# Two transformer layers on one core: which units of the second attention are projected early, in what order the units run, and how the reciprocals of the softmax sums are spread

## The chip, the core and the metric

The kernel runs on one core of one Trainium2 chip. The metric is the device time of one launch in microseconds (us). A core has a matrix engine (PE, with its weight loads shown as PEld), a vector engine (DVE), a scalar engine (ACT), GpSimd (POOL), and SyncE (SP), which here only issues transfers. Each engine runs its instructions in its own order, and they wait for each other by semaphores. Transfers between HBM and the core's memory are issued by SP, ACT or POOL and carried by 16 DMA engines.

## The reference

Everything is fp32. `x` has 8 sequences of 100 tokens with 512 features (800 tokens), the context `ctx` 8 sequences of 722 rows. The two layers, cut to what matters:

```python
# layer 0: attention, 16 heads of 32, causal; keys and values from ctx[:, :100]
y  = softmax(mask(q k^T / sqrt(32))) v ;  x = y @ o_w + o_b (+ the residual)
# FFN 0: layer norm, router over 8 experts, the two best per token
x  = x + sum_of_two( w_e * (gelu(xn W1_e + b1_e) W2_e + b2_e) )
# layer 1: attention, 16 heads of 64; mem = ctx @ Wm serves as keys AND as values
xn = layernorm(x);  q = xn @ Wq;  k, v = split(xn @ Wkv)
k  = concat(k, heads(ctx @ Wm));  v = concat(v, heads(ctx @ Wm))
x  = softmax(q k^T / 8) v @ Wo + bo (+ the residual)
# FFN 1: router over 8 experts, two best, silu(gate) * up, down; then a layer norm
```

In layer 1 each query of 100 sees 100 own keys and 722 projected ones, 822 in all. The product `ctx @ Wm` does not depend on x: it can be computed at any time.

## The kernel before

**Stages.** The 800 tokens lie in 7 tiles of 128 rows. Attention 0 (L445 to 594) runs 32 units (4 groups of four heads times 8 sequences) with keys and scores one unit ahead (`weighed0`, L493; `turned0`, L514; `attended0`, L522), then the output product L585, the residual, the layer norm factors and the router's logits tile by tile. `places` (L218) works out where each token's row goes among the experts' rows, `owners` (L285) reads the experts' order into registers of SP, `by_order` (L291) sorts the biases by that order on DVE (L295, L300). `send` (L303) scatters 14 half tiles of rows from POOL to the HBM table `sent`. FFN0 (`work_off`, L365) fetches the rows of each expert (`xg`, L329), transposes them (L151), multiplies (L656, L341) and writes to the HBM table `answers`; `fetch` (L315, L317) brings each token's two rows back.

**Projections.** A unit of attention 1 is a sequence b and a pair of heads ic (64 units). Its projected memories are mT (128 features by 722), made by `context_columns` (L406: 8 products in two halves of 361, 16 records in the trace at L411, then two ACT copies L415), and mv, the same transposed back by `context_rows` (L417, L423). For the units in EARLY (L32), five each of b = 0 and 1, this is done ahead by `project_early` (L435): those of b = 0 after the routing of FFN0, while the tokens are sent, those of b = 1 after FFN0, while the answers are fetched. The results go to HBM (`kept_keys`, `kept_values`) on ACT's queue. Wm and the context for b = 0 are loaded by SP after routing into tiles of attention 0 that are done with (L609, L611), those for b = 1 by POOL at FFN0's start (`fetch_context`, L637).

**Attention 1** begins with the layer norm and the transposes of its 7 tiles (a loop after the fetch loop), then the queries (L400) and per half the keys (L807). The units then run in order of b and ic, one unit ahead in the scores:

- `keys` (L723) computes mT or, for a kept unit, reads it from HBM by SP; next to a kept unit the first half of the following late one is computed with it;
- `turned` (L766) transposes the probabilities of the unit before, and a POOL copy L782 spreads its reciprocals over 128 columns (`wide`);
- `values` (L734) computes or reads mv;
- `weighed` (L742) makes the scores (L752), the maxima on DVE (L756), exponentials with their sums on ACT (L758), and the reciprocals of the sums (L763);
- `attended` (L785) finishes the unit before: PE transposes `wide` (L788) so that the reciprocals lie along the columns, the 14 pairs of products with mv and v follow (L794), ACT copies the reciprocals out of PSUM (`over`, L796), and DVE multiplies by them (L797).

**What sets the order.** The weights come through a ring of eight 1 MB buffers (class `Weights`, L44): `load(n)` issues on SP the next pieces of a fixed list, in the order of the list, and each waits for its buffer. With `behind`, a one-element POOL copy ties a load to another tile. Within each engine a scheduler arranges instructions by their dependences and its own priorities; buffers go round in pools (the number `bufs` each), and a new tile waits for the readers of the old one in its place.

Of the kernel before, what the change touches and what calls it, by code (L numbers as in the profile page):

```python
# [8 lines left out]
F32 = mybir.dt.float32  # L9
# [4 lines left out]
P = 128  # L14
# [17 lines left out]
EARLY = ((0, 1, 3, 5, 7), (0, 1, 3, 5, 7))  # L32
KEPT = {(b, ic): (b * len(EARLY[0]) + k) for b in range(len(EARLY)) for k, ic in enumerate(EARLY[b])}

# [9 lines left out]
class Weights:  # L44


    def __init__(self, nc, pool, pieces):
        self.nc, self.pool, self.pieces, self.tiles = nc, pool, pieces, []

    def load(self, n, behind=None):  # L50

        while len(self.tiles) < min(n, len(self.pieces)):
            t = self.pool.tile([P, 4, 512], F32, tag="w", name=f"w{len(self.tiles)}")
            piece = self.pieces[len(self.tiles)]
            if behind is not None:
                self.nc.gpsimd.tensor_copy(t[:1, 0, :1], behind[:1, 0, :1])
            self.nc.sync.dma_start(out=t, in_=piece() if callable(piece) else piece)
            self.tiles.append(t)
# [7 lines left out]
def two_layers(ctx: ExitStack, tc: tile.TileContext, a: dict, out: bass.AP):  # L66
# [8 lines left out]

    pieces = [a[n] for n in ("k_w", "q_w", "v_w", "o_w")]
    W_L0F = len(pieces)
# [8 lines left out]
    pieces += [a["Wq"][g] for g in range(2)] + [a["Wkv"][g] for g in range(4)]  # L86
    pieces += [a["Wm"][g] for g in range(2)] + [a["Wo"][g] for g in range(2)]
# [127 lines left out]
    kept_keys = dram.tile([len(KEPT), P, S], F32, name="kept_keys")  # L215
    kept_values = dram.tile([len(KEPT), P, NSC, P], F32, name="kept_values")
# [74 lines left out]
    def by_order(hot, src, n, pool, name):  # L291

        shape = [P, NE, n, NE]
        wide = pool.tile(shape, F32, tag=f"o_{name}", name=f"o_{name}")
        nc.vector.tensor_tensor(  # L295
# [69 lines left out]
    def work_off(jobs, arrive, hidden, product, send_back, first=None, midway=None):  # L365
# [3 lines left out]
        if first is not None:  # L369
            weights.load(first + 8, raw)  # L370
# [35 lines left out]
    def context_columns(mT, ic, cb, w_m, psum, tag, halves=(0, 1)):  # L406

        for h in halves:
            pm = psum.tile([P, 512], F32, tag=tag, name="ps_m")
            for dc in range(DC):  # L410
                nc.tensor.matmul(  # L411
                    pm[:, : S // 2], w_m[ic // 4][:, dc, (ic % 4) * P : (ic % 4 + 1) * P],
                    cb[:, dc, h * (S // 2) : (h + 1) * (S // 2)], start=dc == 0, stop=dc == DC - 1,
# [21 lines left out]
    def project_early(b, cb, w_m, tiles, psum, tags):  # L435
        for ic in EARLY[b]:
            mT, mv = tiles()
            context_columns(mT, ic, cb, w_m, psum, tags[0])
            nc.scalar.dma_start(out=kept_keys[KEPT[b, ic]], in_=mT)
            context_rows(mv, mT, psum, tags[1], nc.scalar.copy)  # L440
            moved(nc.scalar.dma_start, mv, kept_values[KEPT[b, ic]], True)
# [4 lines left out]
    with tc.tile_pool(name="a0", bufs=1) as ap, tc.tile_pool(name="a0w", bufs=3) as aw, tc.tile_pool(  # L446
# [19 lines left out]
        for t in (sent, answers):  # L466
            for r0, r1 in ((0, sum(CAPS)), (sum(CAPS), ROWS)):
                flat = t[r0:r1].rearrange("r d -> (r d)").rearrange("(p f) -> p f", p=P)
                n = (r1 - r0) * D // P
                for k in range(0, n, 1024):  # L470
                    if t is sent or r0:
                        nc.sync.dma_start(out=flat[:, k : min(n, k + 1024)], in_=nil[:, : min(1024, n - k)])

        xT = ap.tile([P, DC, NT], F32, tag="xT", name="xT0")
# [69 lines left out]
        prs, prTs = {}, {}  # L544
        for n in range(len(units) + 2):
            if n < len(units):
# [25 lines left out]
        xT = ap.tile([P, DC, NT], F32, tag="xT", name="xTf0")  # L572
# [31 lines left out]
        weights.load(W_L0F + 2)  # L604
        send(xl, where, "f0")
        w_m = []
        for g, tag in enumerate(("cT", "kT")):
            w_m.append(ap.tile([P, 4, 512], F32, tag=tag, name=f"wm0{g}"))
            nc.sync.dma_start(out=w_m[g], in_=a["Wm"][g])  # L609
        cb = ap.tile([P, DC, S], F32, tag="v", name="cb0")  # L610
        nc.sync.dma_start(out=cb, in_=a["ctxT"][:, 0, :].rearrange("(c p) s -> p c s", p=P))  # L611
        project_early(
            0, cb, w_m, lambda: (
                ap.tile([P, S], F32, tag="nil", name="mT0", bufs=2), aw.tile([P, NSC, P], F32, tag="xn", name="mv0")
            ), ps, ("tp", "av"),
        )
        b1s = by_order(hot, b1.rearrange("p e f -> p f e"), F0 // P, fp, "b1")
        b2s = by_order(hot, b2T, DC, fp, "b2")
# [386 lines left out]
```

## Time and profile before

| | |
|---|---|
| median of 3 runs (lowest, highest) | 1885.26 us (1885.07, 1887.0) |
| the profiled execution | 1887.75 us |
| its span in the trace | 1886.0 us |
| mean granted clock of PE | 0.952 |
| PE busy, matmuls of it at L411 | 1744.2 us, 277.6 us (864 records) |
| DVE, ACT, POOL busy | 576.5, 468.3, 161.7 us |
| moved by DMA | 225.15 MB, 119 GB/s over the span |

The stages by their place in the span (us): head 0 to 41, attention 0 to 158, its output and logits to 203, routing and early projections to 238, wait for FFN0's rows to 255, FFN0 to 639, fetching back with early projections to 680, layer norm to 698, queries and keys to about 780, units of attention 1 to about 1480, FFN1 to 1822, output.

How to read the lines: L12 is line 12 of the kernel. A line of a timeline gives the start, the length of a run of alike instructions, engine, line, operation, result and operands, shape, count, and in brackets how long the engine had been idle and what released it. Matmuls are pipelined, so a run's own length overlaps the next; the distance of two starts is what a slot costs. A row of stages gives busy time and count by engine, the granted clock (1.00 is full), the share of DMA time and GB/s.

### The profile page before, as it was taken

The page shows a single profiled execution, that of the slowest core. Times are in us where ns is not written, and L with a number is a line of the kernel's source. Part 1 is how long each engine was busy: PE and PEld are TensorE (multiplying, and loading weights), DVE is VectorE, ACT ScalarE, POOL GpSimd, SP SyncE. Part 2 cuts the span into 40 slices and gives each one's busy share as a digit, 9 for nine tenths or more (in the row PEclk, how much of TensorE's full clock was granted, in tenths as well). Part 3 has the DMA queues.
Part 4 walks back from the last instruction along what each step waited for, and adds up shares of the span by engine and source line. Part 5 has one row for each costly group of instructions (what it writes and reads, how often), then busy time and mean ns, then how long its engine had stood idle before and what let it go on. Part 6 is the DMA issues. An engine that isn't in the chain of part 4 may idle for free. (4 is left out here: it accounts for less than half of the span.)

```text
span 1886.0 us, 26129 instructions
## 1 busy us (share of the span) xinstructions
PE 1744.2 (92%) x10442; PEld 1318.2 (70%) x10442; DVE 576.5 (31%) x1379; ACT 468.3 (25%) x1389; POOL 161.7 (9%) x281
## 2 busy tenths in 40 slices
PE   5999969999999879999999999999999939999990
PEld 2455559999999745666666666666666428999990
DVE  4465300101111140355444234444443321111115
ACT  2374311111111141343333323333332010010110
POOL 4010110000000130000000000000000140000003
PEclk9997879999999979999999999999999859999995
DMA  9701284464556552032000000000000056555523
GB/s 368 313 24 55 108 317 164 177 248 174 201 205 231 196 176 79 24 95 72 1 32 1 32 1 32 1 33 1 1 1 1 12 199 224 183 181 203 206 89 113
DMA packets 51883, 225.15 MB, mean 119 GB/s; under 512 B 8336, under 2 KB 10008, under 8 KB 35104
## 3 DMA queue, kind: packets, MB, share of 16 engines
q1 hardware_dynamic: 32440, 169.51, 24.8%
q0 software_dynamic: 10064, 32.15, 4.8%
q10 hardware_dynamic: 9240, 21.65, 3.2%
q8 instruction: 86, 1.41, 0.3%
q14 instruction: 53, 0.43, 0.1%
HBM read 176.76 MB, written 46.53 MB: 118 GB/s over the span
## 5 line engine op out<-in xcount | busy, mean ns | idle before, releaser
L341 PE MATMUL ps_y<-h,w 128*128 128x256 f32 (+7 forms) x1536 | 280.5, 344 | 0.0
L411 PE MATMUL ps_m<-cb,w 128*128 128x361 f32 x864 | 277.6, 472 | 0.0
L341 PEld LDWEIGHTS ps_y<-h,w 128*128 128x128 f32 x1536 | 268.6, 190 | 7.9
L411 PEld LDWEIGHTS ps_m<-cb,w 128*128 128x128 f32 x864 | 158.9, 189 | 95.4 <-issue 3.6
L656 PE MATMUL ps_h<-xgT,w 128*128 128x256 f32 (+7 forms) x1024 | 189.9, 347 | 0.0
L656 PEld LDWEIGHTS ps_h<-xgT,w 128*128 128x128 f32 x1024 | 181.0, 192 | 6.0
L758 ACT ACTIVATE pr<-ps_sc,m 100x822 f32<-100x822 f32 x128 | 120.0, 943 | 192.6 <-DVE m L756 192.6
L774 DVE COPY prT<-ps_ptA 128x500 f32<-128x500 f32 x128 | 82.2, 678 | 197.1 <-PE ps_ptA L773 197.1
L756 DVE TENSOR_REDUCE m<-ps_sc 100x1 f32<-100x822 f32 x128 | 123.8, 1009 | 47.2 <-PE ps_sc L752 47.2
L660 ACT ACTIVATE h<-ps_h,s_b 128x256 f32<-128x256 f32 (+7 forms) x128 | 56.2, 439 | 315.6 <-PE ps_h L656 315.6
L415 ACT COPY mT<-ps_m 128x361 f32<-128x361 f32 x128 | 59.0, 462 | 252.1 <-PE ps_m L411 224.3
L400 PE MATMUL ps_col<-xT,w 128*128 128x400 f32 x320 | 115.3, 519 | 0.0
L884 PE MATMUL ps_g<-xgT,w 128*128 128x256 f32 (+7 forms) x512 | 104.6, 348 | 0.0
L884 PE MATMUL ps_u<-xgT,w 128*128 128x256 f32 (+7 forms) x512 | 103.1, 344 | 0.0
L400 PEld LDWEIGHTS ps_col<-xT,w 128*128 128x128 f32 x320 | 61.9, 197 | 46.2 <-issue 4.6
L884 PEld LDWEIGHTS ps_g<-xgT,w 128*128 128x128 f32 x512 | 91.4, 192 | 3.0
L884 PEld LDWEIGHTS ps_u<-xgT,w 128*128 128x128 f32 x512 | 91.1, 191 | 2.8
L752 PE MATMUL ps_sc<-mT,qT 64*100 64x311 f32 (+1 forms) x512 | 91.9, 466 | 0.0
L889 ACT ACTIVATE sg<-ps_g 128x256 f32<-128x256 f32 (+7 forms) x64 | 22.3, 349 | 239.3 <-PE ps_g L884 239.3
L782 POOL COPY wide<-sums 100x128 f32<-100x128 f32 x64 | 18.8, 294 | 728.1 <-DVE sums L763 728.1
L890 DVE TENSOR_TENSOR h<-ps_u,sg 128x256 f32<-128x256 f32 (+7 forms) x64 | 24.4, 381 | 184.2 <-PE ps_u L884 152.9
L794 PE MATMUL ps_av<-prT,mv 128*64 128x100 f32 (+1 forms) x1536 | 80.6, 253 | 0.0
(240 smaller groups left out, 1964.0 us busy)
## 6 DMA issues: line engine op xcount, KB each, us to landing
w<-in_W SPq DMA_DIRECT2D x64, 1024.0 KB
w<-in_w_gate SPq DMA_DIRECT2D x16, 1024.0 KB
w<-in_w_up SPq DMA_DIRECT2D x16, 1024.0 KB
w<-in_w_down SPq DMA_DIRECT2D x16, 1024.0 KB
sent<-nil SPq DMA_DIRECT2D x25, 512.0 KB
cb<-in_ctxT ACTq DMA_DIRECT2D x8, 1444.0 KB
answers<-nil SPq DMA_DIRECT2D x19, 512.0 KB
xg<-sent POOLq DMA_DIRECT2D x18, 256.0 KB, 4.8
```

The lines of the kernel that those rows point to most:

```text
L341: nc.tensor.matmul(py[:, k, :n], ws[f // 4][:, f % 4, dc * P : (dc + 1) * P], h[:, f, :n], start=f == 0, stop=f == nf - 1,)
L400: nc.tensor.matmul(ps[:, :HALF], w[c // 4][:, dc, (c % 4) * P : (c % 4 + 1) * P], xT[:, dc, cols], start=dc == 0, stop=dc == DC - 1,)
L411: nc.tensor.matmul(pm[:, : S // 2], w_m[ic // 4][:, dc, (ic % 4) * P : (ic % 4 + 1) * P], cb[:, dc, h * (S // 2) : (h + 1) * (S // 2)], st ...
L415: nc.scalar.copy(mT[:, h * (S // 2) : (h + 1) * (S // 2)], pm[:, : S // 2])
L656: nc.tensor.matmul(ph[:, :n], w[:, dc, j * P : (j + 1) * P], xg[:, dc, :n], start=dc == 0, stop=dc == DC - 1,)
L660: nc.scalar.activation(h[:, f, :n], ph[:, :n], AF.Gelu, bias=b1s[:, e, f : f + 1])
L752: nc.tensor.matmul(sc[:, bank, c0:c1], qT[r, ic, q0 : q0 + T], keys_, start=True, stop=True)
L756: nc.vector.tensor_reduce(m, sc[:, :, :NKH], AX.XY, ALU.max, negate=True)
L758: nc.scalar.activation(pr.rearrange("p (a n) -> p a n", a=2), sc[:, :, :NKH], AF.Exp, bias=m, accum_out=sums[:, j : j + 1],)
L774: nc.vector.tensor_copy(prT[:, : NSC - 1, :], pt)
L794: nc.tensor.matmul(po[r, 0, :], vj, prT[j][:w, c, :], start=c == 0, stop=c == NSC)
L884: nc.tensor.matmul(p_[:, :n], w_[:, dc, j * P : (j + 1) * P], xg[:, dc, :n], start=dc == 0, stop=dc == DC - 1,)
```

## The change

1. EARLY has 14 units, all 8 of b = 0 and 6 of b = 1, so 50 units are projected in attention 1 where 54 were.
2. `project_early` becomes a generator of three steps per unit (two halves of mT, then mv with the stores). Ten steps of b = 0 are taken in the last ten turns of attention 0's loop, the other 14 after routing. Its stores go to SP's queue. Its inputs are four pieces of the weight ring, loaded at the start.
3. For b = 1, Wm comes from the ring too (order now Wq, Wm, Wkv, Wo); a limit keeps the ring from loading Wkv until the last answers have been fetched. POOL fetches the context in two halves.
4. The layer norm and transposes of attention 1 stand in the loop that fetches FFN0's answers, and the transposed x has a pool of its own.
5. `by_order` is tied behind the places of the second choice by a POOL copy.
6. The reciprocals go through HBM: SP writes the 100 by 2 sums to `shares`, the two heads apart, and reads each back spread over 64 partitions (`over`). The POOL copy, the PE transpose and the ACT copy go.
7. Kept mT and mv are read by POOL's queue.
8. The units run as b = 0 and 2 in turn, then 1 and 3 in turn, then b = 4 to 7; `batch` remembers its context tile, keys and values by b and loads no context for b = 0.

```diff
@@ -29,8 +29,8 @@
...
-EARLY = ((0, 1, 3, 5, 7), (0, 1, 3, 5, 7))
-KEPT = {(b, ic): (b * len(EARLY[0]) + k) for b in range(len(EARLY)) for k, ic in enumerate(EARLY[b])}
+EARLY = ((0, 1, 2, 3, 4, 5, 6, 7), (0, 1, 3, 5, 6, 7))
+KEPT = {u: k for k, u in enumerate((b, ic) for b in range(len(EARLY)) for ic in EARLY[b])}
...
     pieces = [a[n] for n in ("k_w", "q_w", "v_w", "o_w")]
+    W_EARLY = len(pieces)
+    pieces += [a["Wm"][g] for g in range(2)] + [context(0, h) for h in range(2)]
...
-    pieces += [a["Wq"][g] for g in range(2)] + [a["Wkv"][g] for g in range(4)]
-    pieces += [a["Wm"][g] for g in range(2)] + [a["Wo"][g] for g in range(2)]
+    pieces += [a[n][g] for n in ("Wq", "Wm") for g in range(2)]
+    pieces += [a["Wkv"][g] for g in range(4)] + [a["Wo"][g] for g in range(2)]
...
+    shares = dram.tile([B * IC, 2, T], F32, name="shares")
...
-    def by_order(hot, src, n, pool, name):
+    def by_order(hot, src, n, pool, name, behind):
 
         shape = [P, NE, n, NE]
         wide = pool.tile(shape, F32, tag=f"o_{name}", name=f"o_{name}")
+        nc.gpsimd.tensor_copy(wide[:1, 0, 0, :1], behind[:1, :1])
...
-    def project_early(b, cb, w_m, tiles, psum, tags):
+    def project_early(b, cb, w_m, tiles, psum, tags, dma):
+
         for ic in EARLY[b]:
             mT, mv = tiles()
-            context_columns(mT, ic, cb, w_m, psum, tags[0])
-            nc.scalar.dma_start(out=kept_keys[KEPT[b, ic]], in_=mT)
+            for h in range(2):
+                context_columns(mT, ic, cb, w_m, psum, tags[0], (h,))
+                yield
+            dma(out=kept_keys[KEPT[b, ic]], in_=mT)
             context_rows(mv, mT, psum, tags[1], nc.scalar.copy)
-            moved(nc.scalar.dma_start, mv, kept_values[KEPT[b, ic]], True)
+            moved(dma, mv, kept_values[KEPT[b, ic]], True)
+            yield
...
+        weights.load(W_L0F)
...
+        steps = project_early(
+            0, weights.tiles[W_EARLY + 2 : W_L0F], weights.tiles[W_EARLY : W_EARLY + 2], lambda: (
+                ap.tile([P, S], F32, tag="nil", name="mT0", bufs=2), aw.tile([P, NSC, P], F32, tag="xn", name="mv0")
+            ), ps, ("tp", "av"), nc.sync.dma_start,
+        )
         for n in range(len(units) + 2):
+            if n >= len(units) - B:
+                next(steps)
...
         weights.load(W_L0F + 2)
+        for _ in steps:
+            pass
+        b1s = by_order(hot, b1.rearrange("p e f -> p f e"), F0 // P, fp, "b1", where[1])
+        b2s = by_order(hot, b2T, DC, fp, "b2", where[1])
         send(xl, where, "f0")
-        w_m = []
-        for g, tag in enumerate(("cT", "kT")):
-            w_m.append(ap.tile([P, 4, 512], F32, tag=tag, name=f"wm0{g}"))
-            nc.sync.dma_start(out=w_m[g], in_=a["Wm"][g])
-        cb = ap.tile([P, DC, S], F32, tag="v", name="cb0")
-        nc.sync.dma_start(out=cb, in_=a["ctxT"][:, 0, :].rearrange("(c p) s -> p c s", p=P))
-        project_early(
-            0, cb, w_m, lambda: (
-                ap.tile([P, S], F32, tag="nil", name="mT0", bufs=2), aw.tile([P, NSC, P], F32, tag="xn", name="mv0")
-            ), ps, ("tp", "av"),
-        )
-        b1s = by_order(hot, b1.rearrange("p e f -> p f e"), F0 // P, fp, "b1")
-        b2s = by_order(hot, b2T, DC, fp, "b2")
...
-        cb = fp.tile([P, DC, S], F32, tag="xl", name="cb1")
+        cb = fp.tile([P, 2, DC, S // 2], F32, tag="xl", name="cb1")
...
-            for t, src in (
-                (w_m[0], a["Wm"][0]), (w_m[1], a["Wm"][1]),
-                (cb, a["ctxT"][:, 1, :].rearrange("(c p) s -> p c s", p=P)),
-            ):
-                nc.gpsimd.tensor_copy(t[:1, 0, :1], behind[:1, 0, :1])
-                nc.gpsimd.dma_start(out=t, in_=src)
+            for h in range(2):
+                nc.gpsimd.tensor_copy(cb[:1, h, 0, :1], behind[:1, 0, :1])
+                nc.gpsimd.dma_start(out=cb[:, h], in_=context(1, h))
...
+        weights.limit = W_L1A + 4
...
+        bo = fw.tile([P, D], F32, name="bo", bufs=1)
+        nc.scalar.dma_start(out=bo, in_=a["bo"][0].partition_broadcast(P))
+        for _ in project_early(
+            1, [cb[:, h] for h in range(2)], [weights.get(W_L1A + 2 + g, 0) for g in range(2)], lambda: (
                 fw.tile([P, S], F32, tag="xgT", name="mT1"), fw.tile([P, NSC, P], F32, tag="xg", name="mv1")
-            ), ps, ("m", "tp"),
-        )
+            ), ps, ("m", "tp"), nc.scalar.dma_start,
+        ):
+            pass
+        xT1 = columns_tile("xT1")
...
                 nc.vector.scalar_tensor_tensor(
                     x[:w, i, :], y[:w], m[:w, i : i + 1], x[:w, i, :], ALU.mult, ALU.add
                 )
+            xn = fw.tile([P, D], F32, tag="y", name="xn1")
+            scaled(xn, x[:, i, :], *factors(moments(x[:, i, :], "a1"), "b", twice=True))
+            to_columns(xT1, xn, i * P, rows[i], ps, gamma1, beta1)
+            nc.gpsimd.tensor_tensor(x[:, i, :], x[:, i, :], bo, ALU.add)
+        weights.limit = len(pieces)
+        weights.load(W_L1A + 8, y[:1, :1])
...
-        weights.load(W_L1A + 8)
-        xT = ap.tile([P, DC, NT], F32, name="xT1")
-        with tc.tile_pool(name="a1l", bufs=2) as lp:
-            bo = lp.tile([P, D], F32, name="bo", bufs=1)
-            nc.scalar.dma_start(out=bo, in_=a["bo"][0].partition_broadcast(P))
-            for i in range(NTILE):
-                xn = lp.tile([P, D], F32, tag="xn", name="xn1")
-                scaled(xn, x[:, i, :], *factors(moments(x[:, i, :], "a1"), "b", twice=True))
-                to_columns(xT, xn, i * P, rows[i], ps, gamma1, beta1)
-                nc.gpsimd.tensor_tensor(x[:, i, :], x[:, i, :], bo, ALU.add)
-
+        xT = xT1
...
             if (b, ic) in KEPT:
-                nc.sync.dma_start(out=mT, in_=kept_keys[KEPT[b, ic]])
+                nc.gpsimd.dma_start(out=mT, in_=kept_keys[KEPT[b, ic]])
...
             if (b, ic) in KEPT:
-                moved(nc.sync.dma_start, mv, kept_values[KEPT[b, ic]], False)
+                moved(nc.gpsimd.dma_start, mv, kept_values[KEPT[b, ic]], False)
...
             nc.vector.reciprocal(sums, sums)
-            return prs, sums
-
-        def turned(prs, sums):
+            share, over = shares[b * IC + ic], small.tile([P, T], F32, tag="over", name="over1")
+            nc.sync.dma_start(out=share.rearrange("j t -> t j"), in_=sums)
+            for r, j in zip(rows_, range(2)):
+                nc.sync.dma_start(out=over[r], in_=share[j].partition_broadcast(H1))
+            return prs, over
+
+        def turned(prs, over):
...
-            wide = small.tile([T, 2, H1], F32, tag="wide", name="wide1")
-            nc.gpsimd.tensor_copy(wide, sums.unsqueeze(2).to_broadcast([T, 2, H1]))
-            return out, wide
-
-        def attended(b, ic, v, mv, prT, wide):
-
-            po = ps.tile([P, 2, T], F32, tag="tp", name="ps_av1")
-            nc.tensor.transpose(po[:, 1, :], wide.rearrange("t j d -> t (j d)"), ident[:T, :T])
+            return out, over
+
+        def attended(b, ic, v, mv, prT, over):
+
+            po = ps.tile([P, T], F32, tag="tp", name="ps_av1")
             for c in range(NSC + 1):
                 w = min(P, S - c * P) if c < NSC else T
                 for j in range(2):
                     r = slice(j * H1, (j + 1) * H1)
                     vj = mv[:w, c, r] if c < NSC else v[:, ic * P + j * H1 : ic * P + (j + 1) * H1]
-                    nc.tensor.matmul(po[r, 0, :], vj, prT[j][:w, c, :], start=c == 0, stop=c == NSC)
-            over = small.tile([P, T], F32, tag="over", name="over1")
-            nc.scalar.copy(over, po[:, 1, :])
-            nc.vector.tensor_tensor(qT[:, ic, b * T : (b + 1) * T], po[:, 0, :], over, ALU.mult)
-
...
+                    nc.tensor.matmul(po[r, :], vj, prT[j][:w, c, :], start=c == 0, stop=c == NSC)
+            nc.vector.tensor_tensor(qT[:, ic, b * T : (b + 1) * T], po, over, ALU.mult)
...
+        shared = {}
...
+            if b in shared:
+                return shared[b]
+            cb = None
+            if any((b, ic) not in KEPT for ic in range(IC)):
+                cb = aw.tile([P, 2, DC, S // 2], F32, tag="cb", name="cb")
+                for h in range(2):
+                    nc.scalar.dma_start(out=cb[:, h], in_=context(b, h))
+                cb = [cb[:, h] for h in range(2)]
...
                 nc.vector.tensor_copy(v[:, g * 512 : (g + 1) * 512], pv)
-            return cb, kT, v
-
-        before = kT = None
-        for n in range(B * IC):
-            b, ic = divmod(n, IC)
-            if ic == 0:
-                cb, kT, v = batch(b, kT)
+            shared[b] = cb, shared["kT", half], v
+            return shared[b]
+
+
+        units = [(b + 2 * k, ic) for b in range(2) for ic in range(IC) for k in range(2)]
+        units += [(b, ic) for b in range(4, B) for ic in range(IC)]
+        before = None
+        for n, (b, ic) in enumerate(units):
+            cb, kT, v = batch(b)
             mT = keys(b, ic, cb)
-            if (b, ic) in KEPT and ic + 1 < IC and (b, ic + 1) not in KEPT:
-                keys(b, ic + 1, cb, whole=False)
+            if (b, ic) in KEPT and n + 1 < len(units) and units[n + 1] not in KEPT:
+                b_, ic_ = units[n + 1]
+                keys(b_, ic_, batch(b_)[0], whole=False)
```

## The prediction

> **What bounds the kernel now.** First the page's busy shares, then the span cut into its stages, last the timelines of the stages that the change touches. In the first line PE is busy 92% of the span; no other engine passes 31%. In the stages (columns: length, busy time of PE, its weight loads, DVE, ACT, POOL, granted clock, DMA share, GB/s) the work that sets the time shows where PE fills the whole stretch: attention 1 does (895 to 1425). Not filled: 238 to 255, where PE waits 17 us for FFN0's first rows, and 673 to 710, the way from FFN0 to attention 1.
>
> ```profile
> PE 1744.2 (92%) x10442; PEld 1318.2 (70%) x10442; DVE 576.5 (31%) x1379; ACT 468.3 (25%) x1389; POOL 161.7 (9%) x281
> ```
>
> ```profile
> 203.00:238.00 35.00, 34.15 (x128) 21.18 (x128) 11.90 (x58) 10.86 (x26) 10.52 (x11) 0.87 0.47 171
> 238.00:255.00 17.00, 2.64 (x12) 2.27 (x12) 2.12 (x7) 2.20 (x4) 6.83 (x16) 0.55 0.76 281
> ...
> 673.00:710.00 37.00, 24.95 (x82) 15.40 (x82) 12.01 (x30) 15.66 (x45) 8.93 (x8) 0.72 0.44 155
> ...
> 895.00:1425.00 530.00, 530.00 (x3696) 349.22 (x3695) 220.72 (x425) 177.86 (x514) 13.51 (x46) 1.00 0.04 12
> ```
>
> In attention 1 one late unit on PE begins with the L411 projection. It also holds the slot of L788, the transpose that turns the reciprocals:
>
> ```profile
> 1400.43 0.31 PE L788 MATMUL ps_av<-ident,wide 100*128 100x100 f32 x1
> 1400.67 1.25 PE L794 MATMUL ps_av<-prT,mv 128*64 128x100 f32 x24
> 1401.76 0.34 PE L794 MATMUL ps_av<-prT,v 100*64 100x100 f32 x4
> 1402.03 5.12 PE L411 MATMUL ps_m<-cb,w 128*128 128x361 f32 x16
> ```
>
> **Attention 1, the gain.** L411 groups start at 925.75 and 935.97: two late units in a row are 10.22 us apart. A pair early+late takes 14.78 us (789.67 to 804.45), so an early unit is 14.78 - 10.22 = 4.56 us and a projection is 10.22 - 4.56 = 5.66 us of PE. Four more early units: 4 x 5.66 = 22.6 us. The L788 slot is 1400.67 - 1400.43 = 0.24 us; 64 of them go: 15.4 us. Now three places have two early units side by side (about 778, 819 to 826 and 882 to 888), where the period is 6.24 us in place of 4.56 (1.7 more), since the short unit does not cover scores, exponentials and copies of its neighbour. In the new order the 28 units of batches 0 to 3 that hold early ones stand as early, late, early, late almost throughout; two of the three places go: 2 x 1.7, and something at the third, 4 us. Sum: -42 us. DVE, ACT and POOL lose work here (POOL's copy L782, ACT's copy over L796) and are not the limit, so nothing is taken for them. The ten kept reads become fourteen and go from SP to POOL; they land in two buffers a unit ahead, POOL does nothing else then: 0. If a POOL read came late, PE would wait for mT, and a pair would give part of its 5.66 us back.
>
> **The reciprocals through HBM.** In place of a POOL copy, a transpose and an ACT copy, SP writes 200 numbers and, once they have landed, issues two reads. Queued behind that wait on SP is only the next unit's write: the last weight loads of the stage stand before the first of them in SP's order. Who waits is the DVE multiply (L797). In the timeline of DVE:
>
> ```profile
> 806.41 0.17 DVE L763 RECIPROCAL sums<-sums 100x2 f32<-100x2 f32 x1 [1.52 <-ACT pr L758]
> 806.50 0.24 DVE L797 TENSOR_TENSOR qT<-ps_av,over 128x100 f32<-128x100 f32 x1
> ...
> 813.13 0.17 DVE L763 RECIPROCAL sums<-sums 100x2 f32<-100x2 f32 x1 [1.24 <-ACT pr L758]
> 813.21 0.24 DVE L797 TENSOR_TENSOR qT<-ps_av,over 128x100 f32<-128x100 f32 x1
> ```
>
> A unit's reciprocal is ready at 806.5; its multiply runs one period later, at 813.2, and before it DVE has nothing that it holds up until about 813. So the round trip has 6.7 us in an early/late pair (the gaps are 8.07 and 6.72) and 10.2 between late units. The nearest row for its length is the last store of the kernel:
>
> ```profile
> 1882.45 0.69 DVE L933 TENSOR_TENSOR x<-x,acc 128x512 f32<-128x512 f32 x1
> ```
>
> DVE ends at 1883.14 and the span, store landed, at 1886.00: at most 2.86 us from the end of a DVE instruction to landed. Twice that, write and read, is 5.7 us; the store's own DMA events end some 1.7 us after DVE, twice 3.4. A rule of the Trainium skill speaks against this form: by "DMA: Bandwidth & Descriptors", Rules for kernel authors, a transfer whose last dimension is not contiguous falls apart into one descriptor per element and should be rearranged. The write is exactly that, 100 partitions of 2 numbers scattered 400 bytes apart: 200 four-byte pieces against the 32 rows of 2 KB of the row above. By the row 3.4 to 5.7 us, hidden, 0; by the rule the write alone is longer by an amount that no row here shows, and over 6.7 us it would be paid. I take 5 us, hidden, since 200 pieces are few and HBM is nearly idle (12 GB/s in that stage); ends: 0 and the rival below.
>
> **Attention 0's tail.** Ten of the 24 steps of batch 0's projections (3.3 units, 3.3 x 5.66 = 19 us of PE) now stand in its last iterations. There PE is at half clock before: between 141 and 161 the granted clock is 0.50, and eight units take 3.04 us each (141.51 to 144.54), 24.3 us, though PE's slots lie end to end. With column matmuls between the units, at 124.58 to 130.26, the clock is 1.00 and two units with eight such matmuls take 5.68 us; the matmuls' slots are 0.79 + 2.12 of it, so 1.4 us are left per unit. The Trainium skill ("TensorE: Matmul & The Clock Gate", What's actually happening) has the clock at half after one idle window of about 3.4 us and at full after as long a busy one; by that alone PE, occupied from 141 on, would be back at full by 145. The trace says otherwise (20 us at 0.50 with small matmuls; 203.4 to 212.2 even with projections). So: full clock, as at 124 to 130: 8 x 1.4 + 19 = 30.3, +6 us on the way to the router's logits. At half clock throughout it would be 24.3 + 38 - 24.3 = +38 us, which the nearest row (1.00 with fillers) makes unlikely; at best the projections fill what was wait, and the faster output matmuls give 2 us back: +3. I take +7, ends +3 and +13.
>
> **Routing to FFN0.** The rows that count:
>
> ```profile
> 219.46 2.02 DVE L295 TENSOR_TENSOR o_b<-hot_f,p_b 128x1024 f32<-128x1024 f32 x1
> 223.81 1.08 POOL L308 DMA_INDIRECT sent<-xl,whole_f  x1 [62.70 <-DVE pick_f L263]
> 248.11 2.25 POOL L329 DMA_DIRECT2D xg<-sent  x4 [6.21 <-DMA kept_values<-mv]
> 251.69 1.94 PE L151 MATMUL ps_tp<-ident,xg 128*128 128x128 f32 x8 [13.88 <-DMA xg<-sent]
> ```
>
> DVE's ordering of the biases (2.02, and L300's 1.20, with small ones beside them) goes behind the places: -3.5 us for the first send. It comes then at 223.8 + 7 - 3.5, +3.5. The xg read waits for the kept stores (the third row), whose buffers it takes over. 14 steps, 4.7 units, remain after routing against 5 before, and start 7 us later; the stores are now on SP, behind the register loads for the experts (6.6 us from 219.1 to SP's next load at 225.8) and two weight loads of 1 MB, and PE's next unit waits for the buffers of the one stored. With that, FFN0 starts later by 3.5 (the sends) to 12 us; I take +7. The loads for the projections come earlier, through the ring, at the head, where the DMA engines have a whole attention to finish in: 0; without that cover the 3.4 MB would be 9 us at the 393 GB/s of 230 to 238.
>
> **FFN0 to attention 1.** Batch 1 gets six units for five: +5.7 us of PE at 639 to 680. Gone is the wait for its stores:
>
> ```profile
> 684.02 1.00 DVE L140 TENSOR_SCALAR xn<-x,rb,tb 128x512 f32<-128x512 f32 x2 [6.10 <-DMA kept_values<-mv]
> ```
>
> The layer norms run inside the fetch loop, but their buffers hold two tiles and PE has all transposes behind the sixth unit, so five tiles' norms still follow it: the 13.2 us from 684.6 to the first column matmul at 697.84 shrink to about 10. 5.7 - 5 - 3 = -2 us, ends -8 and +2. Wkv loads wait for the last fetch, with 25 us until L806 asks for them: 0. FFN0 inside, FFN1 and the output are untouched: 0.
>
> **Sum.** -42 + 7 - 2 = -37. The profiled execution took 1887.75 us (span 1886.0), so it becomes 1850.8; the median of the runs, 1885.26, is 2.5 lower, so 1848.
>
> **Rivals.**
> - *The front costs nothing*: the tail's projections only fill PE's waits (+3), sends come first (-3.5), stores are in time, and the boundary gives its 8: -42 + 0 - 6, near 1838. For it: PE at half clock in the tail. Against: stores behind SP's loads. 0.15.
> - *The early work merely moves*: three units lengthen the tail by 13 and SP's queue holds the stores, so FFN0 starts 16 to 20 us later; -42 + 18, near 1861. For it: the release of 248.11; against: PE was at half clock. 0.20.
> - *Slower: the round trip is the loop.* Reciprocal, write, read, multiply, next reciprocal stand in one order on DVE. From 6.8 us on each further microsecond is paid by some 28 of the 32 early/late units: at 8.1 us the -37 are used up; at 8.8 us it is +56 - 37, near 1904. For it: 200 small pieces and two waits in series on one queue. Against: 2.86 us for a whole store. 0.10.
>
> **How the numbers follow.** Likeliest, 0.55: 1848, its own ends 1840 and 1856 from the terms' bounds. With the first two rivals 1836 to 1866 holds 8 in 10; the third stays out. A difference of 0.2% (3.8 us) is about what a measurement here can tell from none. Faster: 0.55 + 0.15 + nearly all of 0.20, 0.87; within: 0.03, a round trip near 8 us; slower: 0.10.
>
> **What would show it.** L788's slots gone and late/late at 9.98 us, early+late at 14.3: the main term. Reciprocal to multiply on DVE without idle time released by a DMA: the round trip is hidden; with it, the third rival. The granted clock at 141 to 161 near 1.00, the first send near 227, FFN0's first transposes near 259, and the first column matmul of attention 1 near 703: the front. I am wrong if the half clock stays in the tail, if POOL's reads come late, or if DVE waits for over.

## The result, and the profile after

The changed kernel takes 1953.3 us (median of 4 runs, 1947.6 to 1959.9) where the kernel before takes 1885.6: a ratio of 1.036, 95% interval 1.032 to 1.039. It is slower by 68 us where 37 us less were forecast. The profiled execution took 1959.89 us, its span 1957.9 us.

The page's first section and three stages of the same bounds as before (length, busy time of PE, its weight loads, DVE, ACT, POOL, clock, DMA share, GB/s):

```profile
PE 1747.6 (89%) x10378; PEld 1320.1 (67%) x10378; DVE 571.7 (29%) x1367; ACT 462.6 (24%) x1337; POOL 168.1 (9%) x263
```

```profile
203.00:238.00 35.00, 32.58 (x132) 20.38 (x133) 16.16 (x75) 10.68 (x26) 7.88 (x8) 0.85 0.22 79
238.00:255.00 17.00, 5.39 (x19) 3.13 (x17) 0.00 (x0) 2.65 (x8) 7.54 (x8) 0.68 0.90 348
895.00:1425.00 530.00, 486.14 (x3412) 320.17 (x3411) 208.18 (x393) 161.17 (x444) 12.90 (x24) 0.95 0.23 31
```

In attention 1 PE no longer fills the stretch: 486 of 530 us, with 3412 matmul records where there were 3696. At the head of the list of waits of 800 to 1500 stands DVE's multiply (engine, line, releaser, us in total, times, longest):

```profile
DVE qT L810 <- DMA over<-shares: 202.2, 56, 8.1
```

PE's own wait is before its transposes of the probabilities: by the page 61.6 us in all, and what ended 60.1 of them was DVE, at the reciprocal that directly follows the multiply:

```profile
L791 PE MATMUL ps_ptA<-ident,pr 100*128 100x100 f32 x640 | 82.0, 262 | 61.6 <-DVE sums L777 60.1
```

The timelines of DVE and of SP for one unit in the middle of the stage (start, length, engine, line):

```profile
1008.35 0.26 DVE L810 TENSOR_TENSOR qT<-ps_av,over 128x100 f32<-128x100 f32 x1 [1.61 <-DMA over<-shares]
1008.53 0.15 DVE L777 RECIPROCAL sums<-sums 100x2 f32<-100x2 f32 x1
1011.98 1.28 DVE L792 COPY prT<-ps_ptA 128x500 f32<-128x500 f32 x2 [3.30 <-PE ps_ptA L791]
...
1015.11 1.93 DVE L770 TENSOR_REDUCE m<-ps_sc 100x1 f32<-100x822 f32 x2 [0.70 <-PE ps_sc L766]
1019.58 0.26 DVE L810 TENSOR_TENSOR qT<-ps_av,over 128x100 f32<-128x100 f32 x1 [2.54 <-DMA over<-shares]
1019.76 0.16 DVE L777 RECIPROCAL sums<-sums 100x2 f32<-100x2 f32 x1
```

```profile
1008.71 0.28 SPq L779 DMA_DIRECT2D shares<-sums  x1
1015.00 1.09 SPq L781 DMA_DIRECT2D over<-shares  x2
1019.95 0.28 SPq L779 DMA_DIRECT2D shares<-sums  x1
```

The reciprocal ends at 1008.68, SP issues the write at 1008.71 and can issue the reads only at 1015.00, and DVE has the spread factors at 1019.58. At once after the multiply, DVE takes the next reciprocal, whose sums ACT had finished at 1018.2. That is a closed loop: reciprocal, write, reads, multiply, next reciprocal. The multiply also frees the place in PSUM from which it reads, and PE's next transposes wait for such a place, so PE stops too (the 60.1 us above). Over all units the median from reciprocal to multiply is 10.3 us, 6.1 of it from write to read; the room in an early/late pair was 6.7. From the first reciprocal to the last it took 667 us before (777.7 to 1444.9) and takes 720 us after (795.3 to 1515.2), though four units fewer are projected there. PE's waits come with half clock: the granted clock of 895 to 1425 is 0.95 where it was 1.00 (and is 1.00 again in the version with one read and a later multiply, below). How much of the loss that makes was not separated.

The front, in the lines that answer to those of before:

```profile
228.69 1.07 POOL L317 DMA_INDIRECT sent<-xl,whole_f  x1 [60.83 <-DVE pick_f L271]
...
258.13 2.26 POOL L338 DMA_DIRECT2D xg<-sent  x4 [10.19 <-DMA kept_values<-mv]
262.73 1.94 PE L158 MATMUL ps_tp<-ident,xg 128*128 128x128 f32 x8 [9.09 <-DMA xg<-sent]
```

```profile
706.42 53.99 PE L409 MATMUL ps_col<-xT,w 128*128 128x400 f32 x152 [1.28 <-ACT xT L167]
```

The first send comes 4.9 us later, FFN0's first transposes 11.0, the first column matmuls of attention 1 8.6. Between 141 and 161 the granted clock of PE is now 1.00 where it was 0.50. The row of that stretch, before and after:

```profile
141.00:161.00 20.00, 20.00 (x125) 11.32 (x125) 12.87 (x32) 10.67 (x57) 1.94 (x7) 0.50 0.14 54
```

```profile
141.00:161.00 20.00, 19.66 (x168) 12.18 (x167) 10.90 (x29) 12.23 (x56) 1.47 (x5) 1.00 0.20 75
```

### The profile page after: what moved, and what is told of

Same layout as the page of the kernel before. It is cut to its first block, busy times and chain, and to the rows that moved or that the text cites. A ratio compares the mean times of both kernels' runs of the same rounds, so it can differ in the third digit from the quotient of the medians.

```text
span 1957.9 us, 26224 instructions
## 1 busy us (share of the span) xinstructions
PE 1747.6 (89%) x10378; PEld 1320.1 (67%) x10378; DVE 571.7 (29%) x1367; ACT 462.6 (24%) x1337; POOL 168.1 (9%) x263
## 5 line engine op out<-in xcount | busy, mean ns | idle before, releaser
L420 PE MATMUL ps_m<-cb,w 128*128 128x361 f32 x896 | 290.9, 473 | 0.0
L420 PEld LDWEIGHTS ps_m<-cb,w 128*128 128x128 f32 x896 | 164.2, 189 | 96.0 <-issue 3.4
L791 PE MATMUL ps_ptA<-ident,pr 100*128 100x100 f32 x640 | 82.0, 262 | 61.6 <-DVE sums L777 60.1
L791 PEld LDWEIGHTS ps_ptA<-ident,pr 100*128 100x128 f32 x640 | 68.6, 148 | 84.5 <-issue 70.9
L766 PE MATMUL ps_sc<-mT,qT 64*100 64x311 f32 (+1 forms) x512 | 103.8, 523 | 0.0
L809 PEld LDWEIGHTS ps_av<-prT,mv 128*64 128x64 f32 (+1 forms) x1536 | 70.1, 140 | 46.1 <-issue 46.1
```

The source lines that it names most:

```text
L420: nc.tensor.matmul(pm[:, : S // 2], w_m[ic // 4][:, dc, (ic % 4) * P : (ic % 4 + 1) * P], cb[h][:, dc, : S // 2], start=dc == 0, stop=dc = ...
L766: nc.tensor.matmul(sc[:, bank, c0:c1], qT[r, ic, q0 : q0 + T], keys_, start=True, stop=True)
L791: nc.tensor.transpose(pt[:, c, :], pr[:, T + c * P : T + (c + 1) * P], ident[:T, :T])
L809: nc.tensor.matmul(po[r, :], vj, prT[j][:w, c, :], start=c == 0, stop=c == NSC)
```

## The experiments

Two theories stood at the start. A: the round trip through HBM is the loop of attention 1 and alone makes the loss; the other parts of the change do what they were costed at. B: the new order of units, the kept reads on POOL or the fuller front cost too. The kernel before was timed anew beside each group of runs: 1883.0 us beside the first four below, 1881.9 beside the next four, 1883.9 beside the last four. The ratios are to these runs.

**The reciprocals as before.** The POOL copy, the PE transpose and the ACT copy come back, and the kept reads go to SP:

```diff
-            nc.sync.dma_start(out=share.rearrange("j t -> t j"), in_=sums)
...
+            wide = small.tile([T, 2, H1], F32, tag="wide", name="wide1")
+            nc.gpsimd.tensor_copy(wide, sums.unsqueeze(2).to_broadcast([T, 2, H1]))
...
+            nc.tensor.transpose(po[:, 1, :], wide.rearrange("t j d -> t (j d)"), ident[:T, :T])
```

> The changed kernel with the reciprocals turned as before (POOL copy, PE transpose, ACT copy) and, since SP is free again, the kept reads on SP as before. Theory A (the round trip through HBM alone makes the loss; measured reciprocal to multiply 10.3 us against 6.7 us of room): late/late 10.22 us and early+late 14.8 us as before, four projections and the early/early neighbours fewer (-26.6), the front +8.6 as measured in the changed kernel: about 1868 us. Theory B (the new order of units, the spread kept reads and the fuller front cost too): above 1890 us.

Measured: 1866.4 us, ratio to before 0.991 (0.989 to 0.993). Theory A holds to 2 us: without the way through HBM the change makes the kernel faster by 17 us. The kept reads went back to SP in the same edit, so this run alone doesn't clear POOL of them; the versions further down leave them on POOL and are faster still. PE's L420 groups have the spacing of before, 10.22 us between late units and 14.8 us for an early one with a late one:

```profile
945.21 5.13 PE L420 MATMUL ps_m<-cb,w 128*128 128x361 f32 x16
955.43 5.13 PE L420 MATMUL ps_m<-cb,w 128*128 128x361 f32 x16
965.66 2.70 PE L420 MATMUL ps_m<-cb,w 128*128 128x361 f32 x8
...
980.46 5.13 PE L420 MATMUL ps_m<-cb,w 128*128 128x361 f32 x16
```

**Only the reciprocals through HBM**, in the kernel before. The kept reads go to POOL here too, and the POOL copy, the transpose and the ACT copy go.

```diff
-            return prs, sums
...
+            nc.sync.dma_start(out=share.rearrange("j t -> t j"), in_=sums)
+            for r, j in zip(rows_, range(2)):
+                nc.sync.dma_start(out=over[r], in_=share[j].partition_broadcast(H1))
+            return prs, over
...
```

> The kernel before with only the reciprocals through HBM (and the kept reads on POOL, since SP is taken). Theory A: the loop over DVE and SP gives every unit its period, early or late, some 10.6 us; the 63 periods between first and last multiply grow from 666 to about 720 us, so 1935 to 1945 us. Theory B: only the pairs with an early unit lose, late/late falls to 9.98 us by the transpose saved: below 1900 us.

Measured: 1925.0 us (one run). The loss is there without the rest of the change (+42 us), so B falls as an account of it; but it is 10 us below A's window, and not every unit pays, as A had it. Late units run at 10.0 us (median): in this trace 5.8 us pass from write to read, and where the round trip stays under the late unit's own time it is hidden. The loop bites on the early/late pairs, whose two periods add up to about 20 us and more in place of 14.8: from the first to the 32nd reciprocal it takes 338.6 us for 290.2 before, over the last 32 units 331.5 for 338.4.

**Pieces of 8 bytes.** Half as many pieces in the write. This kernel leaves out the right pairing: the factors reach the wrong tokens, with the same work:

```diff
-            nc.sync.dma_start(out=share.rearrange("j t -> t j"), in_=sums)
+            nc.sync.dma_start(out=share.rearrange("j t -> (j t)").rearrange("(t j) -> t j", j=2), in_=sums)
```

> The changed kernel with the 200 sums written as 100 pieces of 8 bytes in place of 200 of 4 (the pair of one token side by side; read back as before, so the factors come to the wrong tokens: the values differ, the work does not). If the write's 6.1 us are a cost per small piece, half the pieces: write about 3.6 us, round trip about 7.8 us, early/late units near 8.2 us and late units bound by PE at 10: about 1872 us. If they are the price of one write and its completion whatever the pieces: no change, about 1953 us.

Measured: 1860.6 us (one run), some 90 us less than the changed kernel for one different address pattern. SP's timeline:

```profile
1012.62 0.28 SPq L779 DMA_DIRECT2D shares<-sums  x1
1015.35 2.69 SPq L781 DMA_DIRECT2D over<-shares  x2
```

From write to read 2.73 us (both here and in the median) in place of 6.1. So it is the form of the write, not that there are two transfers in series.

**A later multiply.** The loop can also be opened: ACT copies out of PSUM, and DVE multiplies in place, ordered behind the reciprocal of a unit five later.

```diff
...
-            nc.vector.tensor_tensor(qT[:, ic, b * T : (b + 1) * T], po, over, ALU.mult)
+            here = qT[:, ic, b * T : (b + 1) * T]
+            nc.scalar.copy(here, po)
+            owed.append((here, over))
+            if len(owed) > 4:
+                settle()
...
```

> The changed kernel with the multiply taken out of the loop: ACT copies the attended values out of PSUM at once, and DVE multiplies them in place five units later, so that nothing waits for the round trip. Theory A: PE sets the period again, late/late 9.98 and early+late 14.3 us, attention 1 -42, front +8.6: about 1853 us. Rival: SP needs 7.5 us per unit for its write, wait and two reads, more than the 7.15 us that a unit of an early/late pair takes, and is then the loop: each of 28 units +0.4 us and the tail of the stage longer, 1865 us or more.

Measured: 1868.3 us (1866.2 to 1869.1), ratio 0.992 (0.990 to 0.994): the rival's figure. The periods are PE's own (6.7 and 7.6), but SP takes 7.6 us per unit (6.5 from write to read, 1.1 to issue the reads) and falls behind: the write for the reciprocal of 892.55 goes out at 921.08. That is felt where the sequences change. ACT's loads of the next contexts (L835) start only when one of SP's late reads has landed (issued at 909.77, landed at 915.46), and the exponentials stand behind them on ACT:

```profile
915.48 0.38 ACTq L835 DMA_DIRECT2D cb<-in_ctxT  x1
915.95 0.95 ACT L774 ACTIVATE pr<-ps_sc,m 100x822 f32<-100x822 f32 x1 [10.73 <-DMA over<-shares]
```

Four such loads hold ACT for 35 us, and all of the 15 us that this version loses between the first and the last reciprocal against the one with one read and a later multiply, below, lie at the two changes of sequences where they stand. A longer queue hides the latency of the round trip, not the time that it takes of a queue that waits in order.

**One read.** The 8-byte form with the right values: tokens' pairs side by side, one read of 800 bytes to 128 partitions, two multiplies that take every second number.

```diff
...
+            nc.sync.dma_start(out=share, in_=sums)
+            nc.sync.dma_start(out=over, in_=share.partition_broadcast(P))
...
+            for j in range(2):
+                r = slice(j * H1, (j + 1) * H1)
+                nc.vector.tensor_tensor(qT[r, ic, b * T : (b + 1) * T], po[r, :], over[r, :, j], ALU.mult)
```

> The changed kernel with the 8-byte pieces in a form that keeps the values: the sums are written side by side per token (100 pieces of 8 bytes), one read spreads all 200 over 128 partitions, and two DVE multiplies of 64 partitions each take every second one. If the pieces of the write were the cost: as in the run with pairs, write 2.7 us, round trip some 6.5 us, about 1858 us. If the wait is for two transfers in series whatever they carry, the pairs were luck and this stays above 1900 us.

Measured: 1861.6 us (one run). The early/late periods are still 7.4 to 8.2 us, a little above PE's 7.15: the loop is nearly, not wholly, out of the way.

**One read and a later multiply.** The one-read form, with the multiply three units later:

```diff
...
-                nc.vector.tensor_tensor(qT[r, ic, b * T : (b + 1) * T], po[r, :], over[r, :, j], ALU.mult)
+            nc.scalar.copy(qT[:, ic, b * T : (b + 1) * T], po)
+            owed.append((ic, b, over))
+            if len(owed) > 2:
+                settle()
...
```

> The same with the multiply three units later (ACT copies out of PSUM, DVE multiplies in place). SP now needs about 3.6 us a unit, so it can't be the loop as it was in the first version with a later multiply. Theory A: PE sets the period throughout, early+late 14.3 us, no stall near the change from batches 0 and 2 to 1 and 3: about 1850 us. Rival: something else holds the early units (the kept reads on POOL, the ACT copies): 1860 us or more.

Measured: 1852.1 us (median of 4; 1850.8 to 1862.8), ratio to before 0.986 (0.983 to 0.989). This version beats both kernels, the one before by 30 us (1881.9 beside it) and the changed one by some 100. PE's timeline, early+late and late/late:

```profile
927.13 2.70 PE L420 MATMUL ps_m<-cb,w 128*128 128x361 f32 x8
933.89 2.70 PE L420 MATMUL ps_m<-cb,w 128*128 128x361 f32 x8
941.45 5.13 PE L420 MATMUL ps_m<-cb,w 128*128 128x361 f32 x16
951.44 5.13 PE L420 MATMUL ps_m<-cb,w 128*128 128x361 f32 x16
```

933.89 to 941.45 with 927.13 to 933.89 is 14.3 us, 941.45 to 951.44 is 9.99: what the prediction gave for a hidden round trip. That clears the kept reads on POOL and the new order of theory B's charge. From here on this run (1852) is the base.

**The stores on ACT's queue again.**

```diff
-            ), ps, ("tp", "av"), nc.sync.dma_start,
+            ), ps, ("tp", "av"), nc.scalar.dma_start,
```

> As the run before, with batch 0's stores on ACT's queue again. FFN0's first transposes start 11.0 us later in the changed kernel than before, 4.9 us of it by the later sends. If the rest is the stores' place on SP behind the register loads and two weight loads: 5 to 6 us less, about 1845 us, first transposes near 257. If it is the transfers and PE's work behind them: no difference within 2 us.

Measured: 1853.8 us (1852.1 to 1854.7), ratio 0.985 (0.983 to 0.987): no difference. FFN0's first transposes start at 262.3 (260.7 in the base). The stores' place on SP isn't what delays FFN0: it is late with either queue, in a stretch with the DMA engines about 90% busy (0.92 in this trace between 238 and 255). What does delay it shows in the run with five and five early units.

**The units in the old order.**

```diff
-        units = [(b + 2 * k, ic) for b in range(2) for ic in range(IC) for k in range(2)]
-        units += [(b, ic) for b in range(4, B) for ic in range(IC)]
+        units = [(b, ic) for b in range(B) for ic in range(IC)]
```

> As the run of one read and a later multiply, with the units in the old order of sequence and pair. Then eleven early units follow an early one. By the prediction's 1.7 us for each: +17 us, about 1867 us, and early units 6.2 us apart in the first sequence. If early neighbours cost nothing with the transpose gone: no difference.

Measured: 1868.3 us (one run), +16. Most early units in a row are 5.1 to 5.7 us apart (4.3 without transpose if PE set the time). The alternation is worth 16 us with these fourteen units; how the sum divides was not traced further.

**Nothing in attention 0's tail.** All steps of batch 0 after the routing:

```diff
-            if n >= len(units) - B:
-                next(steps)
```

> The run of one read and a later multiply (1852 us) without projections in attention 0's last turns: all 24 steps of batch 0 follow the routing. If the early steps merely move work (they cost 8.4 us on the way to the logits and save as much after the routing): within 3 us of 1852, first send near 220, FFN0's first transposes still near 260. If they fill what attention 0 leaves of PE: 6 us or more slower, since eight projections after routing are 45 us of PE behind 203, and the stores come after them.

Measured: 1867.7 us (1865.1 to 1868.5), ratio 0.992 (0.990 to 0.993): 15.6 us slower than the base (2 of them are the difference between the groups), the second case of the expectation. On POOL:

```profile
219.65 1.07 POOL L317 DMA_INDIRECT sent<-xl,whole_f  x1 [58.69 <-DVE pick_f L271]
...
268.67 2.26 POOL L338 DMA_DIRECT2D xg<-sent  x4 [29.82 <-DMA kept_values<-mv]
```

The tokens are sent 7 us earlier than in the base (226.6), and then everything waits 30 us for the last stored projection. The clock between 141 and 161 is 0.52 again: the early steps in the tail use PE at full clock where it would run at half.

**Five and five early units.**

```diff
-EARLY = ((0, 1, 2, 3, 4, 5, 6, 7), (0, 1, 3, 5, 6, 7))
+EARLY = ((0, 1, 3, 5, 7), (0, 1, 3, 5, 7))
```

> The run of one read and a later multiply with the five and five early units of the kernel before. Four projections come back into attention 1: +22.6 us there. The front gives back what the four cost: by the measured +8.6 us of the changed kernel some 6 to 9 us. Sum: about 1867 us. If the early units cost nothing at the front (the later start has other causes): 1875 us.

Measured: 1863.4 us (1861.3 to 1864.4), ratio 0.989 (0.987 to 0.990), +11.3. Attention 1's first column matmul comes at 691.6, 12.0 us before the base's 703.6, and from there to the last reciprocal it takes 730.9 us for 707.6, +23.3. So four early units bring 23 in attention 1 (22.6 were reckoned) and cost 12 at the front. Most of that is FFN0's start:

```profile
253.04 1.94 PE L158 MATMUL ps_tp<-ident,xg 128*128 128x128 f32 x8 [26.27 <-issue]
...
691.56 8.88 PE L409 MATMUL ps_col<-xT,w 128*128 128x400 f32 x17 [1.27 <-ACT xT L167]
```

FFN0's first transposes come 7.6 us before the base's (260.7), though the first send is no earlier (227.4 for 226.6). It is the three further units of b = 0, wherever their stores are issued, that make FFN0 late.

**Why the write is slow.** A first idea was the number of pieces per DMA engine:

```diff
-            nc.sync.dma_start(out=share.rearrange("j t -> t j"), in_=sums)
+            for t in (slice(0, 96), slice(96, T)):
+                nc.sync.dma_start(out=share.rearrange("j t -> t j")[t], in_=sums[t])
```

> The changed kernel, 200 pieces of 4 bytes as in it, with the write cut into tokens 0 to 95 and 96 to 99. In the trace the write of 100 rows ends with about ten completion events between 4.1 and 5.4 us after its data, which looks like some ten DMA engines that confirm 20 pieces each one after the other, 0.25 us a piece. If 96 rows are spread over sixteen engines, 12 pieces each, write to read falls from 6.1 to about 4.3 us in spite of a transfer more, and the time to about 1905 us. If the number of pieces per engine is not what counts, write to read stays at 6 us or grows, and the time stays near 1953 us.

Measured: 1985.9 us (one run); from write to read 6.7 us (median):

```profile
1012.41 0.71 SPq L780 DMA_DIRECT2D shares<-sums  x2
1018.86 1.09 SPq L782 DMA_DIRECT2D over<-shares  x2
```

The idea falls. In the trace the landing of the 96 rows is told by 16 events, that of the 100 rows in one write by 10, so the pieces are spread wider; yet the same 200 pieces to the same 800 bytes take as long and a little more. The place they go to may count. A trial write in each unit of the version with the reciprocals as before tells:

```diff
...
+            spot = (
+                close[unit].rearrange("j t -> t j"), apart[unit, :, :, 0],
+                close[unit].rearrange("j t -> (j t)").rearrange("(t j) -> t j", j=2), apart[unit, :, 0, :2],
+            )[how]
+            nc.sync.dma_start(out=spot, in_=sums)
+            nc.sync.dma_start(out=seen, in_=spot[:1, :1])
...
```

> The version with the reciprocals turned as before (1866 us), with a trial write that nobody needs in each unit: SP writes the sums to HBM in one of four ways in turn and then reads one number back, so that the trace shows the time from write to read. Ways: 200 pieces of 4 bytes side by side, as in the changed kernel; 200 pieces of 4 bytes, each in a row of 512 bytes of its own; 100 pieces of 8 bytes side by side; 100 pieces of 8 bytes, 1024 bytes apart. If the number of pieces is the cost: about 6.1, 6.1, 2.7 and 2.7 us. If small pieces that fall into one stretch of memory wait for each other: about 6.1, then 2 to 2.5, 2.7, and 2 to 2.5 us. The time of the kernel itself: within 5 us of 1866.

Measured: 1867.7 us as a whole (one run), and on SP (L787 the write, L789 the read; first a pair of the close 4-byte form, then one of the spread 4-byte form, one of close and one of spread 8-byte pieces):

```profile
794.43 0.32 SPq L787 DMA_DIRECT2D close<-sums  x1
800.22 0.24 SPq L789 DMA_DIRECT2D seen<-close  x1
...
816.07 0.86 SPq L787 DMA_DIRECT2D apart<-sums  x1
818.42 0.24 SPq L789 DMA_DIRECT2D seen<-apart  x1
...
822.79 0.29 SPq L787 DMA_DIRECT2D close<-sums  x1
825.51 0.21 SPq L789 DMA_DIRECT2D seen<-close  x1
...
837.58 0.27 SPq L787 DMA_DIRECT2D apart<-sums  x1
838.90 0.21 SPq L789 DMA_DIRECT2D seen<-apart  x1
```

Medians of 16 each: 200 pieces of 4 bytes side by side 5.82 us; the same, each in 512 bytes of its own, 2.15 us; 100 pieces of 8 bytes side by side 2.72 us; 1024 bytes apart 1.33 us. Small pieces side by side in one stretch of HBM are what makes the write dear, as if they waited for each other; their number alone costs little (2.15 against 1.33, and 0.5 of that is SP's longer issue). The spread pieces also start at multiples of 512 bytes of their table, so these trials don't part distance from alignment.

## Why the prediction was wrong, step by step

- **The reciprocals through HBM: the step that failed.** The prediction took "5 us, hidden" for the round trip and put it at 0 in the sum; it came to about +100 us (1953.3 against 1852.1 with the round trip out of the way). The 5 us were from the row of the kernel's last store (1.7 to 2.86 us from DVE to landed, twice). Measured: 10.3 us, 6.1 us from write to read and 4.0 us from the issue of the reads to the multiply. The row was of another kind: 32 rows of 2 KB, where this write is 200 pieces of 4 bytes in 800 bytes. The prediction named the rule of the Trainium skill that speaks against the form ("DMA: Bandwidth & Descriptors", Rules for kernel authors: one descriptor per element) and set it aside with "200 pieces are few and HBM is nearly idle". Both are true, and neither is what counts: by the trial writes, 200 pieces apart take 2.15 us, side by side 5.82.
- **The third rival was the right mechanism**, with the right threshold: it gave +28 us for each us over 6.8. At 10.3 us that is +98 us. Between first and last reciprocal the changed kernel takes 101 us more than the version with one read and a later multiply: 102 over the first 32 units, where the early ones are, 3 over the late sequences, and 4 less at the change between them. So it was the early/late units that paid, as the rival had it. With the -37 its sum is +61; measured +68. Its chance of 0.10 was too small: the only row near it was not of its kind, so the bound from above was no bound. Of the prediction's three signs of being wrong this is the one that came: the clock did rise in the tail, and PE waited for no kept read.
- **Attention 1 without the loop** was costed at -42 us. In the version with the loop opened the way from the first column matmul to the last reciprocal is 707.6 us against 747.0, -39.4. Of this the projections are 23.3 (22.6 reckoned; by five and five early units), and 16.1 are the transposes and the early neighbours together (19.4 reckoned); with the transposes back, the first reciprocal to the last takes 14.7 us more (633.3 for 618.6). The early neighbours cost 16 us if the new fourteen are left in the old order, where 4 us were reckoned for the old ten.
- **Attention 0's tail**: reckoned +7 to the logits; the last logits reach DVE at 215.4 for 207.0, +8.4. The clock went to 1.00 there, as the row of 124 to 130 said and not as by half clock throughout. **The order of the biases**: the first send came 4.9 us later with the logits 8.4 us later, so -3.5, as reckoned.
- **FFN0's start**: +7 reckoned, +11.0 measured, within its ends of 3.5 and 12. The reason was only half right: the register loads and weight loads ahead of the stores on SP were named, and putting the stores on ACT's queue changes nothing; three units of b = 0 fewer bring 7.6 us back. The row of 238 to 255 was read as 17 us of waiting; PE was busy 2.64 us of them, and its line has a wait of 13.88. **FFN0 to attention 1**: -2 reckoned, -2.4 measured (11.0 to 8.6).
- **The second rival**, that the early work merely moves, is not what happened: without the tail's steps the kernel is some 14 us slower.

What remains open: why small pieces side by side in HBM take so long is not visible in a trace of the core, nor whether their distance or their alignment counts. The four forms show that the place does, and not the number.

## What to carry to other kernels

Before a small result takes the way through HBM to be rearranged, look at the form of the write, not at its bytes: measure one write of that very form from issue to the instruction that waits for it, and compare with the room that the loop's shortest period leaves, since a multiply that stands before the next unit's reciprocal on an engine turns the latency into the period. If the way is kept, write pieces that are neighbours in one partition together, read once, and place the consumer some units later; here that made of +68 us a gain of 30. A row of the trace bounds a cost only if it is of the same kind, so a cost without a row of its kind deserves a wide range on the side where it hurts.

## What the runs showed of the hardware that was not expected

- 200 pieces of 4 bytes written to one stretch of 800 bytes in HBM took 5.82 us from issue to the next instruction that waits; 2.15 us when each had 512 bytes of its own; 100 pieces of 8 bytes 2.72 and 1.33 us. The Trainium skill ("DMA: Bandwidth & Descriptors", Specifications) says that transfers under 512 bytes are done by reading, changing and writing back; no run here shows whether that happens. Pieces of 8 bytes spread out were confirmed in 1.33 us, so the smallness of a piece alone doesn't make it dear.
- PE's half clock lasted 20 us (141 to 161 before, 0.50) with its slots end to end, and went when projections stood between the small matmuls (1.00 in the same place after, 0.52 with the tail's projections left out).
